# Small row blocks of the last attention layer: a second buffer for their distances, loads ahead of other steps, zeros written once, values copied a unit later

## The chip, the cores and the metric

The kernel runs on one core of one Trainium2 chip. The metric is the device time of one execution in microseconds (us), taken as the median of several runs. Beside it there is one execution recorded by the hardware profiler; durations, waits and line numbers below come from it.

## The reference, cut to what matters

The network has four layers, each of the form x = x + s * silu(g), with s from a sequence mixer and g from a feed-forward part, both fed with the layer norm of x. The kernel treats 4 sequences of 1024 tokens with 128 features. Only the last layer's code is changed (and where constants are kept), so this is the part to see:

```python
xn = _layernorm(x)
# attention, 16 heads of 8, b sequences of n tokens
qx, kx, vx = split_head(xn @ Wq.T), split_head(xn @ Wk.T), split_head(xn @ Wv.T)
ns = jnp.arange(n) + (MAXLEN - n)                    # MAXLEN = 256
ex = rel_embed[ns].reshape(n, NH, HD).transpose(1, 0, 2)
srel = srel_skew(jnp.einsum('bhnd,hmd->bhnm', qx, ex))
qk = (jnp.einsum('bhnd,bhmd->bhnm', qx, kx) + srel) * inv_dim
atten = jax.nn.softmax(qk - 1e9 * jnp.triu(jnp.ones((n, n)), 1), axis=-1)
s = jnp.einsum('bhnm,bhmd->bhnd', atten, vx).transpose(0, 2, 1, 3).reshape(b, n, d) @ Wp.T + bp
# feed-forward, 384 hidden, weights dequantised by 1/127
g = _silu((silu(xn @ wg.T) * (xn @ wu.T)) @ wd.T)
x = x + s * g
```

srel_skew shifts row n of its argument so that the entry for query n and key m depends on the embedding of their distance n - m. The position embedding has only 256 rows, so that only a band of distances needs a product of its own; the rest has one row in common.

## The kernel before, in words

The first three layers fill the span up to about 2160 us and are touched only where their constants come from. The last layer (`layer3`) runs from there to the end.

Its work is cut into units. A unit is one of 4 sequences, one group of 4 heads (i, of 4 groups) and one block of 128 query rows (t, of 8). The blocks of a group run in the order `ORDER3`, so big blocks (t over 3, with 640 to 1024 keys) and small ones (128 to 512 keys) take turns; there are 128 units, 8 to a head group. A unit's keys are cut into column tiles of 512: two for a big unit, one for a small one.

For a unit the stages are these:

- `relative3`: TensorE multiplies q with the embedding (L1914), ScalarE copies the result r out of PSUM (L1916), SyncE's queue stores it in DRAM as "flat" (L1919, L1920). This is done in parts, one part per unit, seven units ahead (`part(n + 7)`).
- `shear3`: SyncE's queue loads "flat" back with a slanted access pattern (L1935 or L1937, and L1941 for t of 3 and more), so that each row lies at its distances. GpSimd then fills what lies outside with affine selects (L1945), 1 to 3 per unit. The result is the tile "rel", with 4 heads by up to 5 blocks of 128. It is called by `ahead(n + 3)`, three units ahead. Big units take "rel" from a pool of two buffers (`p2`), small ones from a pool of one (`p1`).
- `scores3`: TensorE multiplies q and k into the score tile in PSUM (L1978), of which there is one. VectorE adds rel, scales and takes the row minimum, head by head (L1986 for columns without rel, L1993 with). ScalarE takes the exponential and the row sums (L2000).
- `transpose`: VectorE turns the weights (L1737) into "wT".
- `weigh3`: TensorE multiplies them with the values "vb" (L2014). At a group's end `finish3` scales by the row sums, and at a sequence's end `end3` projects, updates x and stores the output.

The main loop at the end of `layer3` writes the order out by hand: for each column tile the products of a later tile, pending transposes, one step of weighing, the compare of this tile; at a unit's last tile the steps listed after `continue`. Among these, `next(beside, None)` takes one step of what runs beside the attention: the gated feed-forward of the same sequence (`ffn3`: gate and up products L1861, silu L1865, copy of up L1866, their product h on GpSimd L1867, down-projection L1871, g L1872), in head group i = 1, or the beginning of the next sequence (`begin3`: layer norm, projection to q, k, v and their stores), from the fourth unit of i = 2 on. `ahead(n + 3)` comes last.

`project3` loads q and k of the next head group, into tiles of a pool of two, after a memset of q's zero column on GpSimd (L1881). `values3` loads the values as "vr" and copies them into the block-diagonal "vb" on GpSimd (L1899, four copies); `vb` is one tile, so the copies wait until the old group's last weighing has read it. Each engine carries out its instructions in the order in which they are issued, and SyncE's queue does so with DMA issues: one that waits holds back those behind it.

The constants come as one array, one transfer, in a tile kept for the whole kernel.

Of the kernel before, what the change touches and what calls it, by code (L numbers as in the profile page):

```python
# [10 lines left out]
F32 = mybir.dt.float32  # L11
# [8 lines left out]
P = 128  # L20
NB = 4
T = 1024
# [7 lines left out]
def _constants():  # L30
    i = np.arange(P)
    row, col = i[:, None], i[None, :]
    parts = []
# [4 lines left out]

    parts.append(("ident", np.eye(P)))
    parts.append(("tri", row <= col))  # L40
# [5 lines left out]

    parts.append(("sel3", (row // 32 == col // 8 % 4) & (row // 8 % 4 == col // 32)))
    parts.append(("of_a", (row // 8 % 4) == np.arange(4)[None, :]))
    parts.append(("of_t", (row % 8) == np.arange(8)[None, :]))
# [14 lines left out]
    pick = np.zeros((P, 8, P))  # L64
# [3 lines left out]
    at, where = 0, {}  # L68
# [6 lines left out]
CONST, CONST_AT = _constants()  # L75
# [12 lines left out]
def drain(gen):  # L88
    for _ in gen:
        pass  # L90


class Kit:


    def __init__(self, tc, const, const_sb):
        self.tc, self.nc = tc, tc.nc
        self.const_sb = const_sb
        self.n_copy = 0
        self.ident = self.c("ident")  # L100
        self.ident16 = const.tile([P, P], BF16, tag="ident16", name="ident16")
        self.nc.vector.tensor_copy(self.ident16, self.ident)
        self.pick = const.tile([24, 8, P], BF16, tag="pick", name="pick")

    def c(self, name):
        at, n = CONST_AT[name]
        return self.const_sb[:, at : at + n]
# [1564 lines left out]
def layer3(k, W, x3, out, eps5, ps):  # L1672
# [11 lines left out]
    nc, tc = k.nc, k.tc  # L1684
    with ExitStack() as st:
# [16 lines left out]
        def ahead(n):  # L1702
            if n < len(units):
                t = units[n][2]
                rels[n] = shear3(k, p2 if t > 3 else p1, flats[n // 8, t // 2], t)
# [5 lines left out]
        batch[0] = {}  # L1711
# [9 lines left out]
        weights, transposes, weighs, out_of = {}, [], [], {}  # L1721
# [19 lines left out]
        def weigh(n):  # L1741
            nonlocal values
            b, i, t = units[n]
            at, pair = n // 8, t // 2
            if n % 8 == 2:
                out_of[at] = ps.tile([P, 8, 32], F32, tag="o", name="po")
            o = out_of[at]
            yield from weigh3(k, weights.pop((at, pair)), vb, o, pair)
            if n % 8 == 7:
                drain(values)  # L1750
                if i == 0:
                    batch[b]["on"] = p1.tile([P, 4, 256], F32, tag="on", name="on")
                finish3(k, p1, ps, o, group[at]["sums"], batch[b]["on"][:, i, :])
                if i == 3:
                    end3(k, W, temp, ps, x3, b, batch[b], out[b])
            yield
# [12 lines left out]
        for x, (n, first) in enumerate(tiles + [(len(units), 0)] * 4):  # L1769
# [16 lines left out]
            if pos == 3 and i == 2 and b + 1 < NB:  # L1786
                batch[b + 1] = {}
                beside = begin3(k, W, p1, p2, temp, ps, dram, x3, b + 1, eps5, batch[b + 1])
# [6 lines left out]
            if pos == 6 and at + 1 < 4 * NB:  # L1795
                values = values3(k, p1, batch[(at + 1) // 4], vb, (at + 1) % 4)
                next(values)
            next(beside, None)
            ahead(n + 3)
# [76 lines left out]
def project3(k, p2, seq, i, group):  # L1876

    nc = k.nc
    q = p2.tile([P, 1 + T], F32, tag="q", name="q")
    kk = p2.tile([P, T], F32, tag="k", name="k")  # L1880
    nc.gpsimd.memset(q[:, 0:1], 0.0)  # L1881
# [192 lines left out]
def tile_kernel(ctx: ExitStack, tc: tile.TileContext, I, out):  # L2074

    nc = tc.nc
    const = ctx.enter_context(tc.tile_pool(name="const", bufs=1))
    n_const = CONST_AT["pick"][0]
    const_sb = const.tile([P, n_const], F32, tag="const_sb", name="const_sb")
    nc.sync.dma_start(out=const_sb, in_=I["const"][:, 0:n_const])  # L2080
    k = Kit(tc, const, const_sb)
# [4 lines left out]
    whole = ExitStack()  # L2086
    xp = whole.enter_context(tc.tile_pool(name="x", bufs=1, side="right"))
# [57 lines left out]
```

## Time and profile before

| what | value |
|---|---|
| median of 3 runs | 3271.13 us (3264.41 to 3277.84) |
| the profiled execution | 3261.59 us, its span 3259.9 us |
| mean granted TensorE clock | 0.734 of full speed |
| PE busy, whole span | 2317.2 us (71%) |
| VectorE busy, whole span | 2307.1 us (71%) |
| ScalarE busy, whole span | 1487.5 us (46%) |
| GpSimd busy, whole span | 1174.5 us (36%) |
| selects L1945 | 288 of 637 ns |
| memset L1881 | 16 of 99 ns |
| copies of values L1899 | 64 of 1033 ns |

A line of the timeline gives the start in us from the span's start, the duration of the group of instructions, the engine and line, the operation, what it writes and reads, the shape and the count; in brackets stands how long the engine had been idle and what ended that. "SPq" is SyncE's queue, where the duration is that of issuing a transfer. A line of the waits gives who waited for whom, the total in us, how often, and the longest. "issue" is idle time for which the trace shows no cause.

### The profile page before, as it was taken

To read this page: it belongs to the slowest core of one execution; us is meant where nothing else is said; L and a number is where in the kernel's file an instruction comes from. 1 tells how busy PE (TensorE), PEld (TensorE's weight loads), DVE (VectorE), ACT (ScalarE), POOL (GpSimd) and SP (SyncE) were. 2 spreads that over 40 slices of the span, in tenths; PEclk is the share of its full clock that TensorE was granted. 3 is DMA by queue.
4 is the path that set the end of the run, shared out by engine and by line. 5 is a ranking of instruction groups with operands and counts; after the bars stand their busy time and mean duration, and the time that the engine had idled before them with its cause. 6 is when DMAs were issued, how large, how long until landed. Compare 5 with 4: busy or idle time off the path is not lost. (4 is left out here: it accounts for less than half of the span.)

```text
span 3259.9 us, 50636 instructions
## 1 busy us (share of the span) xinstructions
PE 2317.2 (71%) x18321; PEld 1327.2 (41%) x18321; DVE 2307.1 (71%) x5534; ACT 1487.5 (46%) x3248; POOL 1174.5 (36%) x1104
## 2 busy tenths in 40 slices
PE   5787777677776777965533772557888888888885
PEld 2555555222322323651101222344545555555553
DVE  5555545878878886657868878437678778777786
ACT  4555453433333334344322561125665665755663
POOL 3344334144444444224577222332322322323322
PEclk9888888678788888985555666566766766756676
DMA  3000000100000000320433444347677677766772
GB/s 89 3 1 1 1 1 1 35 0 0 0 0 1 0 0 33 105 84 0 111 95 105 109 108 99 110 119 209 187 213 207 181 209 217 202 195 193 200 231 71
DMA packets 396446, 303.46 MB, mean 93 GB/s; under 512 B 96272, under 2 KB 380812, under 8 KB 390564
## 3 DMA queue, kind: packets, MB, share of 16 engines
q1 hardware_dynamic: 395044, 296.03, 32.2%
q10 hardware_dynamic: 1152, 4.19, 0.4%
q8 instruction: 144, 2.36, 0.3%
q14 instruction: 106, 0.87, 0.1%
HBM read 160.63 MB, written 138.94 MB: 92 GB/s over the span
## 5 line engine op out<-in xcount | busy, mean ns | idle before, releaser
L2000 ACT ACTIVATE neg<-neg,low 128x640 f32<-128x640 f32 (+7 forms) x512 | 390.0, 763 | 153.9 <-DVE low L1993 153.8
L1945 POOL TENSOR_SCALAR_AFFINE_SELECT rel<-rel 128x512 f32<-128x512 f32 x288 | 179.9, 637 | 565.6 <-DMA rel<-flat 357.3
L1737 DVE STREAM_TRANSPOSE wT<-neg 128x640 f32<-128x640 f32 (+7 forms) x512 | 362.0, 753 | 7.6 <-ACT neg L2000 6.9
L1978 PE MATMUL score<-k,q 8*128 8x512 f32 (+3 forms) x1536 | 295.0, 747 | 91.2 <-DVE low L1993 91.0
L1993 DVE CUSTOM_DVE_ANT_0 neg<-score,rel,low 128x128 f32<-128x128 f32 (+3 forms) x448 | 217.5, 516 | 152.5 <-PE score L1978 105.6
L1914 PE MATMUL pr<-emb,q 8*128 8x256 f32 x1024 | 245.2, 569 | 45.0 <-ACT r L1916 27.2
L2014 PEld LDWEIGHTS po<-wT,vb 128*32 128x32 f32 x10240 | 208.1, 140 | 143.3 <-issue 78.0
L2014 PE MATMUL po<-wT,vb 128*32 128x64 f32 (+1 forms) x10240 | 242.9, 259 | 31.7 <-issue 17.3
L1914 PEld LDWEIGHTS pr<-emb,q 8*128 8x128 f32 x1024 | 153.6, 269 | 124.4 <-ACT r L1916 62.9
L1916 ACT COPY r<-pr 128x512 f32<-128x512 f32 x256 | 138.4, 581 | 144.2 <-PE pr L1914 95.1
L1993 DVE CUSTOM_DVE_ANT_0 neg<-score,rel 128x512 f32<-128x512 f32 (+3 forms) x320 | 149.3, 520 | 26.7 <-issue 15.4
L1978 PEld LDWEIGHTS score<-k,q 8*128 8x128 f32 x1536 | 103.0, 249 | 153.9 <-DVE low L1993 127.8
L835 PE MATMUL pg<-xnT,w 128*128 128x512 f32 x256 | 148.4, 663 | 7.7 <-DVE h L839 4.5
L214 PE MATMUL pt<-ident,three 128*24 128x128 bf16 x64 | 9.2, 295 | 201.9 <-DVE three L211 201.9
L788 POOL TENSOR_TENSOR prod<-rest,kv 128x2048 f32<-128x2048 f32 x32 | 145.6, 4599 | 18.4 <-ACT rest L778 18.4
L837 PE MATMUL pu<-xin,w 128*128 128x512 f32 x256 | 140.5, 632 | 14.3 <-DVE h L839 7.9
L826 PE MATMUL po<-h,w 128*128 128x512 f32 x256 | 129.6, 627 | 27.1 <-DVE h L839 27.1
L838 ACT ACTIVATE h<-pg 128x512 f32<-128x512 f32 x128 | 75.9, 595 | 156.2 <-PE pg L835 152.7
L1986 DVE TENSOR_SCALAR_CACHE_REDUCE neg<-score 128x384 f32<-128x384 f32 (+2 forms) x192 | 79.7, 415 | 69.3 <-PE score L1978 69.3
L1050 PE MATMUL ph<-xin,upT 128*128 128x512 bf16 (+1 forms) x128 | 71.3, 588 | 78.5 <-DVE xin L1044 77.7
L1455 PE MATMUL read<-kt,const_sb 128*128 128x128 f32 x256 | 50.1, 366 | 94.2 <-POOL kt L1450 94.2
L431 PE MATMUL px<-hT,xbcT 128*128 128x512 f32 x256 | 115.4, 595 | 0.0
(621 smaller groups left out, 5690.5 us busy)
## 6 DMA issues: line engine op xcount, KB each, us to landing
flat<-r SPq DMA_DIRECT2D x256, 256.0 KB
rel<-flat SPq DMA_DIRECT2D x112, 512.0 KB
flat<-r SPq DMA_DIRECT2D x256, 128.0 KB
rel<-flat SPq DMA_DIRECT2D x96, 256.0 KB
kt<-kd SPq DMA_DIRECT2D x16, 512.0 KB
qt<-qd SPq DMA_DIRECT2D x16, 512.0 KB
kdc<-kdd SPq DMA_DIRECT2D x16, 512.0 KB
ktc<-ktd SPq DMA_DIRECT2D x16, 512.0 KB
```

The costliest lines, as they stand in the source:

```text
L788: nc.gpsimd.tensor_tensor(prod, attn.rearrange("p (t h g) -> p t h g", t=4, g=16)[:, t].unsqueeze(2).to_broadcast(each), kv[:, t, 1, :].re ...
L826: nc.tensor.matmul(po, W["w2"][:, e, c, :], h[:, c, :], start=(e == 0 and c == 0), stop=(e == 7 and c == 1))
L835: nc.tensor.matmul(pg, W["w1"][:, e, c * P : (c + 1) * P], xnT, start=True, stop=True)
L837: nc.tensor.matmul(pu, W["w3"][:, e, c * P : (c + 1) * P], xin, start=True, stop=True)
L1737: nc.vector.transpose(weights[at, pair][j][:, t % 2, 0 : (t + 1) * P], S[j][:, 0 : (t + 1) * P])
L1914: nc.tensor.matmul(to[:, m, :], q[at, t * P : (t + 1) * P], W["emb"][at, i, :], start=True, stop=True)
L1916: nc.scalar.copy(r[:, n], to)
L1945: nc.gpsimd.affine_select(out=rel[:, :, slot(back), :], in_=rel[:, :, slot(0), :], compare_op=op, fill=fill, base=0, pattern=[[0, 4], [-si ...
L1978: nc.tensor.matmul(sc[:, j, 0 : last - first], q[at(j), 1 + t * P : 1 + n], kk[at(j), first:last], start=True, stop=True)
L1993: nc.vector.tensor_tensor_reduce(out=neg[:, begin:last], in0=sc[:, j, begin - first : last - first], in1=rel[:, j, slot : slot + (last - b ...
L2000: nc.scalar.activation(neg[:, 0:n], neg[:, 0:n], AF.Exp, bias=here, scale=-1.0, accum_out=group["sums"][:, j, t : t + 1])
L2014: nc.tensor.matmul(o[32 * j : 32 * j + 32, 2 * pair + m.start : 2 * pair + 2, :], vb[:, kb, j].rearrange("p a d -> p (a d)"), weights[j][: ...
```

## The change

It has five parts.

- The constants are put in another order and loaded in two transfers. The first 268 columns, which the last layer needs, stay for the whole kernel (`last_sb`). The other 1080 columns lie in the pool of x, which is given back ahead of the last layer.
- Small units take "rel" from the pool of two buffers as well.
- q has two fixed tiles (`qs`); their zero column is written once, at the start of the layer.
- `ahead(n + 3)` is called before `next(beside, None)` rather than after it.
- The copies of the next group's values are no longer issued where the old group's last weighing ends, but kept in a list (`ripe`) and issued at the end of the current unit, behind `ahead` (or when the next group's weighing starts).

```diff
@@ -36,17 +36,18 @@
         a = np.asarray(a, np.float32)
         return np.ascontiguousarray(np.broadcast_to(a.reshape(1, -1), (P, a.size)))
 
+
     parts.append(("ident", np.eye(P)))
+
+    parts.append(("sel3", (row // 32 == col // 8 % 4) & (row // 8 % 4 == col // 32)))
+    parts.append(("of_a", (row // 8 % 4) == np.arange(4)[None, :]))
+    parts.append(("of_t", (row % 8) == np.arange(8)[None, :]))
     parts.append(("tri", row <= col))
     parts.append(("neg_ssd", np.where(col >= row, 0.0, -1e30)))
     parts.append(("tril", col < row))
     parts.append(("bd8", np.kron(np.eye(16), np.ones((8, 8)))))
     parts.append(("bd16", np.kron(np.eye(8), np.full((16, 16), 1.0 / 16.0))))
     parts.append(("ones", np.ones((P, P))))
-
-    parts.append(("sel3", (row // 32 == col // 8 % 4) & (row // 8 % 4 == col // 32)))
-    parts.append(("of_a", (row // 8 % 4) == np.arange(4)[None, :]))
-    parts.append(("of_t", (row % 8) == np.arange(8)[None, :]))
     parts.append(("sel16", (row // 16) == np.arange(8)[None, :]))
 
     parts.append(("rep8", np.where(row < 8, (col % 8) == row, 0.0)))
@@ -93,9 +94,9 @@
 class Kit:
 
 
-    def __init__(self, tc, const, const_sb):
+    def __init__(self, tc, const, const_sb, last_sb):
         self.tc, self.nc = tc, tc.nc
-        self.const_sb = const_sb
+        self.const_sb, self.last_sb = const_sb, last_sb
         self.n_copy = 0
         self.ident = self.c("ident")
         self.ident16 = const.tile([P, P], BF16, tag="ident16", name="ident16")
@@ -104,7 +105,8 @@
 
     def c(self, name):
         at, n = CONST_AT[name]
-        return self.const_sb[:, at : at + n]
+        n_last = CONST_AT["tri"][0]
+        return self.last_sb[:, at : at + n] if at < n_last else self.const_sb[:, at - n_last : at - n_last + n]
 
     def copy(self, out, in_):
 
@@ -1702,13 +1704,16 @@
         def ahead(n):
             if n < len(units):
                 t = units[n][2]
-                rels[n] = shear3(k, p2 if t > 3 else p1, flats[n // 8, t // 2], t)
+                rels[n] = shear3(k, p2, flats[n // 8, t // 2], t)
 
         def stream():
             for n, (b, i, t) in enumerate(units):
                 yield from scores3(k, p1, p2, ps, group[n // 8], rels.pop(n), t)
 
-        batch[0] = {}
+        qs = [p1.tile([P, 1 + T], F32, tag=f"q{n}", name="q") for n in range(2)]
+        for q in qs:
+            nc.gpsimd.memset(q[:, 0:1], 0.0)
+        batch[0] = {"qs": qs}
         drain(begin3(k, W, p1, p2, temp, ps, dram, x3, 0, eps5, batch[0]))
         group[0] = {}
         drain(project3(k, p2, batch[0], 0, group[0]))
@@ -1718,7 +1723,12 @@
         for n in range(3):
             ahead(n)
         beside, project, values = iter(()), iter(()), iter(())
-        weights, transposes, weighs, out_of = {}, [], [], {}
+        weights, transposes, weighs, out_of, ripe = {}, [], [], {}, []
+
+        def fill_values():
+
+            while ripe:
+                drain(ripe.pop())
 
         def transpose(n, heads):
 
@@ -1739,15 +1749,15 @@
                 weighs.append((big, weigh(n)))
 
         def weigh(n):
-            nonlocal values
             b, i, t = units[n]
             at, pair = n // 8, t // 2
             if n % 8 == 2:
+                fill_values()
                 out_of[at] = ps.tile([P, 8, 32], F32, tag="o", name="po")
             o = out_of[at]
             yield from weigh3(k, weights.pop((at, pair)), vb, o, pair)
             if n % 8 == 7:
-                drain(values)
+                ripe.append(values)
                 if i == 0:
                     batch[b]["on"] = p1.tile([P, 4, 256], F32, tag="on", name="on")
                 finish3(k, p1, ps, o, group[at]["sums"], batch[b]["on"][:, i, :])
@@ -1784,7 +1794,7 @@
             if pos == 0 and i == 1:
                 beside = ffn3(k, W, p1, temp, ps, batch[b])
             if pos == 3 and i == 2 and b + 1 < NB:
-                batch[b + 1] = {}
+                batch[b + 1] = {"qs": qs}
                 beside = begin3(k, W, p1, p2, temp, ps, dram, x3, b + 1, eps5, batch[b + 1])
             if pos == 0:
 
@@ -1795,8 +1805,9 @@
             if pos == 6 and at + 1 < 4 * NB:
                 values = values3(k, p1, batch[(at + 1) // 4], vb, (at + 1) % 4)
                 next(values)
+            ahead(n + 3)
+            fill_values()
             next(beside, None)
-            ahead(n + 3)
         while weighs:
             step()
 
@@ -1876,9 +1887,8 @@
 def project3(k, p2, seq, i, group):
 
     nc = k.nc
-    q = p2.tile([P, 1 + T], F32, tag="q", name="q")
+    q = seq["qs"][i % 2]
     kk = p2.tile([P, T], F32, tag="k", name="k")
-    nc.gpsimd.memset(q[:, 0:1], 0.0)
     group.update({"q": q, "k": kk, "sums": p2.tile([P, 4, NT], F32, tag="sums", name="sums")})
     for n, dst in ((0, q[:, 1:]), (1, kk)):
         for j in range(4):
@@ -2075,16 +2085,18 @@
 
     nc = tc.nc
     const = ctx.enter_context(tc.tile_pool(name="const", bufs=1))
-    n_const = CONST_AT["pick"][0]
-    const_sb = const.tile([P, n_const], F32, tag="const_sb", name="const_sb")
-    nc.sync.dma_start(out=const_sb, in_=I["const"][:, 0:n_const])
-    k = Kit(tc, const, const_sb)
+    whole = ExitStack()
+    xp = whole.enter_context(tc.tile_pool(name="x", bufs=1, side="right"))
+    n_last, n_const = CONST_AT["tri"][0], CONST_AT["pick"][0]
+    last_sb = const.tile([P, n_last], F32, tag="last_sb", name="last_sb")
+    nc.sync.dma_start(out=last_sb, in_=I["const"][:, 0:n_last])
+    const_sb = xp.tile([P, n_const - n_last], F32, tag="const_sb", name="const_sb")
+    nc.sync.dma_start(out=const_sb, in_=I["const"][:, n_last:n_const])
+    k = Kit(tc, xp, const_sb, last_sb)
     eps5 = const.tile([P, 1], F32, tag="eps5", name="eps5")
     nc.vector.memset(eps5, 1e-5)
     store = ctx.enter_context(tc.tile_pool(name="x3", bufs=1, space=DRAM))
     x3 = store.tile([P, NB * NT, D], F32, tag="x3", name="x3")
-    whole = ExitStack()
-    xp = whole.enter_context(tc.tile_pool(name="x", bufs=1, side="right"))
     x_all = xp.tile([P, NB * NT, D], F32, tag="x_all", name="x_all")
 
     right = ExitStack()
```

## The prediction

> **What bounds the kernel now.** First the totals of the fourth layer's stretch (busy time of PE, weight load, VectorE, ScalarE, GpSimd, then granted clock, DMA share, GB/s):
>
> ```profile
> 2200.00:3260.00 1060.00, 875.55 (x13307) 549.51 (x13305) 809.56 (x2556) 628.43 (x1478) 295.66 (x418) 0.68 0.67 193
> ```
>
> No engine is full: PE is busy 83%, VectorE 76%, GpSimd 28%. So the waits of the same stretch come next (engine and its instruction, what it waited for: us, times, longest):
>
> ```profile
> SPq L1935 <- DVE low L1993: 226.9, 81, 11.0
> SPq L1937 <- DVE low L1993: 31.8, 12, 4.9
> ...
> POOL rel L1945 <- DMA rel<-flat: 357.3, 73, 15.5
> ...
> DVE neg L1993 <- PE score L1978: 111.3, 59, 9.7
> PE score L1978 <- DVE low L1993: 91.0, 85, 10.6
> ...
> POOL q L1881 <- PE score L1978: 49.4, 10, 7.8
> POOL h L1867 <- ACT up L1866: 46.9, 26, 8.1
> ...
> DVE neg L1993 <- issue: 42.5, 18, 6.8
> ...
> PE pr L1914 <- ACT r L1916: 27.0, 27, 3.9
> ...
> DVE neg L1993 <- POOL rel L1945: 13.9, 1, 13.9
> ```
>
> Read them by who needs whom. PE's scores and VectorE's compare wait for each other (111.3 and 91.0 us: one PSUM buffer), and that loop sets the pace. SP's load of distances waits 258.7 us for a compare to free its buffer, and GpSimd's select waits 357.3 us for loads, but the compare waited for a select once: 13.9 us, in the first unit of the layer, which this change does not reach. GpSimd idles because its next work isn't there; the path does not go through it.
>
> **Is the select ever late?** I set each select's end against the start of the compare that reads it, unit by unit. After the first unit the slack is never below 2.4 us; the median is 8.2 for small units (t up to 3), 16.7 for big ones. The closest, unit 37:
>
> ```profile
> 2503.97 0.46 SPq L1935 DMA_DIRECT2D rel<-flat  x1
> 2508.56 1.34 POOL L1945 TENSOR_SCALAR_AFFINE_SELECT rel<-rel 128x512 f32<-128x512 f32 x2 [13.49 <-DMA rel<-flat]
> 2512.34 0.56 DVE L1993 CUSTOM_DVE_ANT_0 neg<-score,rel 128x384 f32<-128x384 f32 x1 [2.15 <-issue]
> ```
>
> Load issued at 2503.97, both selects done at 2509.90, compare at 2512.34: slack 2.44 us. The last line's 2.15 us have no cause in the trace, and not the select.
>
> **The change part by part.**
>
> *Second buffer for small units.* Before, the load for unit n+3 waited until unit n+1 had been compared; now it needs n-1's end and never stands. Small units' part of the 258.7 us is some 121 us of SP. Gain on the path: 0, since the selects it makes earlier were 2.4 us early at worst. If that cover were gone, a late select would cost its lateness one to one. Behind these waits on SP stand the stores of r (L1919, L1920). They leave earlier, and ScalarE's copy of r (L1916), whose buffer they free, waited for them 3.3 us in all: I credit 0, with 3 as the other end. At "Best Practices" in the Trainium skill's page Trainium Kernel Development and Optimization stands: double-buffer, so that transfers overlap compute. It would credit this edit with up to the 121 us. The row speaks otherwise: three loads are in flight already and the compare waited for none after the first. By the rule 3271 - 121 = 3150; by the row 3271. I take the row.
>
> *Memsets.* 16 of 0.099 us become 2. GpSimd stood 49.4 us at this memset (for the old scores to be done with q), but behind it stood only selects with slack and the products h, which wait for ScalarE (46.9 us). Gain 0 (bound 2).
>
> *Copies of values a unit later.* Four of 1.03 us per group move from the group's end behind the selects that `ahead` issues. Nobody waited for them: they ended about 4.3 us after the old group's last product, and the new group's first product came at least 6.3 us later. A unit lasts about 8 us (64.5 us for a group of 8), so part of the slack of the tightest groups (3 and 7) is eaten. But the wait they had at GpSimd (76.3 us for PE's products) is gone too. Cost 0, at most 4 x 1.03 in two groups, 8.
>
> *Loads and selects ahead of the other steps.* The steps are the gated FFN (four per batch, in its second head group) and the next batch's beginning. Counts do not change: 208 load issues, 288 selects. On SP the small loads (0.4 to 0.5 us, two for t = 3) now precede a step's x and qk transfers, which have most of a group to spare. On GpSimd the products h now stand behind selects. The FFN's first step, before (issue lines and start, duration, engine):
>
> ```profile
> 2532.91 0.51 SPq L1935 DMA_DIRECT2D rel<-flat  x1
> ...
> 2535.65 0.94 ACT L1866 COPY up<-pgu 128x256 f32<-128x256 f32 x3
> ...
> 2536.12 2.10 POOL L1867 TENSOR_TENSOR h<-h,up 128x256 f32<-128x256 f32 x3 [2.19 <-ACT up L1866]
> ...
> 2538.16 1.94 POOL L1945 TENSOR_SCALAR_AFFINE_SELECT rel<-rel 128x512 f32<-128x512 f32 x3
> 2538.27 1.16 PE L1871 MATMUL po<-downT,h 128*128 128x128 f32 x8 [0.20 <-POOL h L1867]
> 2540.57 0.50 PE L1978 MATMUL score<-k,q 8*128 8x128 f32 x8
> ```
>
> After, the built order is h, two selects, h, one select, h, so the third h comes 3 x 0.64 = 1.9 us later, less some 0.6, because ScalarE's order becomes h, up, h, up and the first product starts sooner. PE's last down-projection follows about 1.3 us later, and so do the scores at 2540.57 queued behind it, for which the next compare waits. The FFN's second step is bound by PE and ScalarE and takes back a part: +0.8 us net per batch, in three batches, +2.4 (0 to 2.5 each, 0 to 7.5). That needs unit 42's load to be in by then: issued at 2532.91 before, earlier after, with some 3 us to land, it is in before the first up. Steps two and three find selects whose loads came long ago. At step four the three products stand behind unit 47's select; its load follows stores of r that are out well before the up copies at 2574, 4 us of room: 0.
>
> *Batch 0.* The units after its second group's start see another order on PE: the next scores stand ahead of the FFN's products rather than behind, which removes a VectorE gap of 4.6 us at unit 12 and gives most of it back at the next tile: -2.7 (-5 to 0).
>
> *Start of the next batch.* In the third group, VectorE's transposes now stand ahead of the layer norm's statistics:
>
> ```profile
> 2631.34 0.74 DVE L1737 STREAM_TRANSPOSE wT<-neg 128x256 f32<-128x256 f32 x2
> 2631.41 5.44 PE L2014 MATMUL po<-wT,vb 128*32 128x64 f32 x201 [0.54 <-DVE ln_mv L137]
> ...
> 2639.30 0.48 DVE L1993 CUSTOM_DVE_ANT_0 neg<-score,rel,low 128x256 f32<-128x256 f32 x1 [2.46 <-PE score L1978]
> ```
>
> PE's stream of weighted sums starts earlier by the 0.26 + 0.17 + 0.26 + 0.17 us of statistics and what goes with them, about 0.9, and the scores behind it as well, for which VectorE stood 2.46 us: -0.9 in each of three batches, -2.7 (-3 to 0). Behind the statistics waits the normalising of x, which has until the next batch.
>
> *Constants in two transfers.* One more issue of 0.4 us on SP ahead of all other loads: +0.4 (0 to 1).
>
> Sum: 2.4 - 2.7 - 2.7 + 0.4 = -2.6 us. The profiled execution took 3261.59 us (span 3259.9, 1.7 around it), so about 3259. The runs' median, 3271.13, lies 9.5 above it, so I forecast 3271.1 - 2.6 = 3268.5, stated as 3268.
>
> **Rivals.**
>
> *Faster: SP's blocked queue is a hidden brake.* For it: 258.7 us of waits in the one queue that also carries the stores, and two rows whose cause may be late loads or stores: compares of small units that waited for nothing visible (15.1 of the 42.5 us "issue") and PE's projections waiting for ScalarE's r (27.0). Against: selects with 2.4 us of slack, and 3.3 us of r waiting for stores. All of it recovered would be 42 us, 3229; half of it, 3250, is this rival's time.
>
> *Slower: a product h stuck behind a select whose load has not landed.* GpSimd is in order, so the down-projection waits, and PE's scores behind it, and the compare. It decides where the load lands after ScalarE's up copies: later than 2535.9 for unit 42, later than 2574.5 for unit 47. Then a step loses what the four stores ahead (4 x 0.5), the landing (3.0) and two selects (1.3) leave: some 6 us, once per batch, 24: 3295. Against it: on the old timeline the loads are 2 to 4 us ahead, and the freed SP queue should widen that.
>
> *The loads do not move.* SP is in order, and its stores wait 146.7 us for ScalarE's r; the loads may sit behind these instead. The edits then do nothing: 3271.
>
> **How the numbers follow.** Forecast 0.57, loads that do not move 0.13, faster 0.14, slower 0.16. A measurement of this kernel tells 0.5% (16 us) from no change; the first two cases lie inside: faster 0.14, same 0.70, slower 0.16. The range runs from the faster rival's 3250 to just under the slower one's, 3293, leaving out half of each; the forecast's own range, with the ends of the sums (-13 to +17, most unlikely together), is 3258 to 3280.
>
> **What would show it.** Right: SP's waits at L1935 and L1937 for the compare fall by about half; the memset's 49.4 us vanish; small units' selects end a unit's length (8 us or so) earlier before their compare; PE's and VectorE's waits for each other stay within a few us of 111 and 91; groups with FFN steps change by 1 or 2 us. Wrong: L1871 waiting for h far above its 16 + 2.4 us (the slower rival), or VectorE's idle time in the layer down by tens of us (the faster one).

## The result: 0.43% slower

The changed kernel takes 3277.07 us (median of 20 runs, 3265.78 to 3285.65), the kernel before 3260.82 us in the same series (median of 20, 3252.27 to 3278.53). The ratio is 1.0043, with a 95% interval of 1.0029 to 1.0057: some 14 us slower (the two medians themselves lie 16.3 us apart). The profiled execution took 3272.36 us, its span 3270.2 us, 10.3 more than before.

TensorE does no more work than before. The totals of the changed kernel's last layer, in the columns of the first line of the prediction:

```profile
2200.00:3270.00 1070.00, 874.22 (x13311) 548.27 (x13308) 809.25 (x2556) 630.39 (x1480) 294.98 (x404) 0.69 0.70 192
```

It is busy 874.2 us (875.6 before) and idle 195.8 us (184.5 before), so what was added is idle time.

The waits of the changed kernel in the last layer, which starts at the same place and ends some 10 us later (line numbers are shifted by 10: L1945 is the load of distances, L2003 the compare, L1988 the scores, L2024 the weighed sums, L1878 the products h). First SyncE's queue, then the engines:

```profile
SPq L1945 <- DVE low L2003: 172.9, 54, 11.2
```

```profile
POOL rel L1955 <- DMA rel<-flat: 394.8, 70, 15.3
DVE neg L2003 <- issue: 129.1, 57, 8.8
...
PE score L1988 <- DVE low L2003: 92.9, 78, 11.7
...
PEld po L2024 <- issue: 90.6, 105, 3.4
...
POOL h L1878 <- ACT up L1877: 33.7, 21, 8.6
DVE neg L2003 <- POOL rel L1955: 31.3, 6, 15.4
PE pr L1924 <- ACT r L1926: 27.0, 25, 4.0
...
PE po L2024 <- issue: 24.4, 18, 3.3
...
DVE neg L2003 <- PE score L1988: 10.2, 11, 2.2
```

What was meant to happen did: SyncE's wait for the compare fell from 258.7 to 172.9 us, the memset's wait is gone, and small units' selects end 18.7 us (median) ahead of their compare rather than 8.2, after the first unit never less than 7.9. None of that shortened the time. The row of compares that waited for a select (31.3 us) is no late select beyond its longest wait, 15.4 us in the first unit of the layer: before each of the other five compares the scores had ended only 0.16 to 0.18 us earlier, so they had waited for the scores. Two rows moved that the reading of the profile before had passed over.

First, the compare's wait changed its name. Before, it was 111.3 us for TensorE's scores and 42.5 without a cause; now it is 10.2 and 129.1, and the 15.9 us of those five compares belong to it too. The sum is nearly the same (153.8 and 155.2), so this looks like bookkeeping. The compare's own view says what it is. Of the kernel before:

```profile
L1993 DVEq EVENT_SEMAPHORE  x198: 21/21/7165, 2194.8 to 3232.7; - x198
```

and of the kernel after (instruction of VectorE's sequencer, count, duration ns min/median/max):

```profile
L2003 DVEq EVENT_SEMAPHORE  x237: 21/330/9328, 2195.9 to 3242.0; - x119
```

These are waits put into instructions of their own, since a compare in the built program carries one wait at most. Before, most of them are over at once (median 21 ns): where a compare waits long for the scores, it mostly does so itself. After, they last (median 330 ns): the wait for the scores has moved into them, and the compare carries its wait for GpSimd. That costs time. From the end of the last score product to the start of a compare that had waited for it over 0.5 us, the median is 69 ns before (75 cases) and 165 ns after (74 cases).

Second, TensorE stands longer where the trace gives no cause, between two weighed sums. That row was "PE po L2014 <- issue: 17.3, 19, 1.9" before; it is 24.4 us, with single gaps up to 3.3. The largest gap, in unit 52 (timeline of the kernel after):

```profile
2637.78 1.33 PE L2024 MATMUL po<-wT,vb 128*32 128x64 f32 x79
2642.40 0.32 PE L2024 MATMUL po<-wT,vb 128*32 128x64 f32 x9 [3.29 <-issue]
2642.65 0.71 PE L1988 MATMUL score<-k,q 8*128 8x256 f32 x8
2643.29 1.58 PE L2024 MATMUL po<-wT,vb 128*32 128x32 f32 x102
2643.54 0.48 DVE L2003 CUSTOM_DVE_ANT_0 neg<-score,rel,low 128x256 f32<-128x256 f32 x1 [2.23 <-PE score L1988]
```

and the transfers from 2636 to 2643 us (busy tenths and GB/s in 40 slices of 0.175 us, then packets by queue):

```profile
DMA  9225788999999999999999999611001100000000
GB/s 47 18 105 176 146 246 211 339 404 392 383 357 345 360 336 325 278 228 301 195 154 115 124 143 116 54 12 18 7 10 10 10 12 1 0 0 0 0 0 0
...
q8 instruction: 1, 0.02, 1.4%
```

Queue 8 brings TensorE's instructions: over the whole kernel it moves 144 packets of 16 KB (2.36 MB), 64 bytes for each of TensorE's some 36,900 instructions. In this window it brings one, from 2639.18 to 2640.80, as the burst of loads ends; TensorE runs dry at 2639.1 and goes on at 2642.4, when the transfers have been quiet for over a microsecond. All gaps of this kind over 0.6 us in the last layer (17 in the kernel after) end 1.2 to 1.7 us after such a packet. Counted in TensorE's instructions they lie a multiple of 256 apart, within one, and 256 instructions of 64 bytes are a packet of 16 KB.

### The profile page after: what moved, and what is told of

It is laid out like the page before. It is cut to its first block, busy times and chain, and to the rows that moved or that the text cites. A ratio compares the mean times of both kernels' runs of the same rounds, so it can differ in the third digit from the quotient of the medians.

```text
span 3270.2 us, 50707 instructions
## 1 busy us (share of the span) xinstructions
PE 2314.5 (71%) x18319; PEld 1325.2 (41%) x18321; DVE 2308.7 (71%) x5534; ACT 1487.9 (45%) x3248; POOL 1175.1 (36%) x1090
## 3 DMA queue, kind: packets, MB, share of 16 engines
q8 instruction: 144, 2.36, 0.3%
## 5 line engine op out<-in xcount | busy, mean ns | idle before, releaser
L1747 DVE STREAM_TRANSPOSE wT<-neg 128x640 f32<-128x640 f32 (+7 forms) x512 | 361.0, 753 | 13.4 <-ACT neg L2010 7.5
L1988 PE MATMUL score<-k,q 8*128 8x512 f32 (+3 forms) x1536 | 291.9, 746 | 93.5 <-DVE low L2003 92.9
L2003 DVE CUSTOM_DVE_ANT_0 neg<-score,rel,low 128x128 f32<-128x128 f32 (+3 forms) x448 | 218.0, 517 | 164.0 <-issue 118.3
L2024 PE MATMUL po<-wT,vb 128*32 128x64 f32 (+1 forms) x10240 | 239.8, 257 | 38.7 <-issue 24.4
L2024 PEld LDWEIGHTS po<-wT,vb 128*32 128x32 f32 x10240 | 205.7, 139 | 150.4 <-issue 90.6
L2003 DVE CUSTOM_DVE_ANT_0 neg<-score,rel 128x512 f32<-128x512 f32 (+3 forms) x320 | 149.3, 521 | 22.8 <-issue 10.9
L1988 PEld LDWEIGHTS score<-k,q 8*128 8x128 f32 x1536 | 101.5, 250 | 154.3 <-DVE low L2003 126.5
L1457 PE MATMUL read<-kt,last_sb 128*128 128x128 f32 x256 | 49.3, 362 | 94.3 <-POOL kt L1452 94.3
```

What stands on the lines that cost most here:

```text
L1747: nc.vector.transpose(weights[at, pair][j][:, t % 2, 0 : (t + 1) * P], S[j][:, 0 : (t + 1) * P])
L1988: nc.tensor.matmul(sc[:, j, 0 : last - first], q[at(j), 1 + t * P : 1 + n], kk[at(j), first:last], start=True, stop=True)
L2003: nc.vector.tensor_tensor_reduce(out=neg[:, begin:last], in0=sc[:, j, begin - first : last - first], in1=rel[:, j, slot : slot + (last - b ...
L2024: nc.tensor.matmul(o[32 * j : 32 * j + 32, 2 * pair + m.start : 2 * pair + 2, :], vb[:, kb, j].rearrange("p a d -> p (a d)"), weights[j][: ...
```

## The experiments

Times are ratios to the kernel before on the same chip in the same series, with 95% intervals. "Standing" is TensorE's row for weighed sums without a cause (17.3 us before, 24.4 after), "step" the median from scores to waiting compare. Both come from one profile each. The single execution that a profile shows lies anywhere in the spread of its runs (some 20 us), so the ratio decides and the rows only name the place. The granted clock does not tell the kernels apart: averaged over its runs it is 0.735 for the kernel before and the one after, 0.736 for a_buffer and 0.734 for a_order.

| kernel | small buffers | ratio | standing us | step ns |
|---|---|---|---|---|
| b_const | 1 | 0.9996 (0.9982 to 1.0011) | 18.6 | 70 |
| a_buffer | 1 | 1.0004 (0.9990 to 1.0017) | 16.9 | 69 |
| b_small_late | 1 | 1.0014 (1.0004 to 1.0024) | 16.1 | 69 |
| before_touch2 | 1 | 1.0002 (0.9987 to 1.0018) | 17.8 | 68 |
| after | 2 | 1.0043 (1.0029 to 1.0057) | 24.4 | 165 |
| a_order | 2 | 1.0036 (1.0025 to 1.0047) | 28.6 | 165 |
| a_fix | 2 | 1.0035 (1.0022 to 1.0047) | 22.3 | 164 |
| b_const_buffer | 2 | 1.0053 (1.0038 to 1.0068) | 28.4 | 165 |
| a_small_late | 2 | 1.0029 (1.0018 to 1.0041) | 20.9 | 165 |
| a_small_early | 2 | 1.0062 (1.0042 to 1.0081) | 17.0 | 165 |
| a_hold | 2 | 1.0077 (1.0050 to 1.0104) | 23.3 | 164 |
| a_touch2 | 2 | 1.0036 (1.0023 to 1.0049) | 22.9 | 68 |
| a_fix_touch2 | 2 | 1.0027 (1.0013 to 1.0041) | 21.9 | 68 |
| a_no_small | 2, hardly used | 1.0000 (0.9985 to 1.0015) | 10.3 | 164 |
| b_dummy | 1 | 1.0151 (1.0124 to 1.0178) | 34.9 | 163 |
| a_touch | 2 | 1.0139 (1.0113 to 1.0166) | 19.5 | 68 |
| before_touch | 1 | 1.0129 (1.0105 to 1.0153) | 15.0 | 68 |

### Which part of the change: four single edits

*a_buffer*: the kernel after with one buffer for small units.

```diff
-                rels[n] = shear3(k, p2, flats[n // 8, t // 2], t)
+                rels[n] = shear3(k, p2 if t > 3 else p1, flats[n // 8, t // 2], t)
```

> The kernel after, but small units take their distances from the pool of one buffer again; everything else of the change stays. Theory 1 (the second buffer makes the selects of the big unit 42, 74, 106 ready so early that they are built in between the three products h of the first feed-forward step, which delays the down-projection and the scores behind it): most of the loss goes, ratio to before 1.0000 to 1.0015. Theory 2 (the order of loads and steps does it, as the prediction had it): the loss stays, 1.0035 to 1.0050. Theory 3 (neither: shifted phases of the TensorE clock and the start of the layer): anything, but the products h uninterrupted.

Measured 1.0004: the loss is gone. The constants, the order of the calls, the fixed q tiles and the later copies of values are all still in, so together they cost nothing that can be measured.

*a_order*: the kernel after with the steps called ahead of the loads again.

```diff
-            ahead(n + 3)
-            fill_values()
             next(beside, None)
+            ahead(n + 3)
+            fill_values()
```

> The kernel after, with the step beside (feed-forward, next batch's beginning) called ahead of the loads again, as before the change. Theory 1 (second buffer): the products h stay interrupted by selects and the loss stays, ratio to before 1.0035 to 1.0050. Theory 2 (order): the loss goes, 1.0000 to 1.0015.

Measured 1.0036: the loss stays. In the built program GpSimd's and ScalarE's order are the same as after, the products h still interrupted by selects; with one buffer (a_buffer) they are not interrupted, though the calls stand as after. So this interruption, which the prediction put down to the order of the calls, is the second buffer's doing; presumably, unit 42's load no longer stands behind unit 41's, its selects are ready sooner, and they are built in ahead of h.

*a_fix*: the kernel after, with h uninterrupted.

```diff
+            if i == 0 and pos == 7:
+                fill_values()
+            elif i == 1 and pos == 0:
+                next(beside, None)
+                ahead(n + 2)
+                ahead(n + 3)
+                fill_values()
+            else:
                 ahead(n + 3)
                 fill_values()
                 next(beside, None)
```

> The kernel after with one thing more: at the start of the second head group, where the first feed-forward step stands, the load and the selects of the unit two ahead are issued behind that step and not one unit earlier, so that GpSimd multiplies h three times without a select in between. Second buffer, order, memsets and copies of values stay. Theory 1: most of the loss goes, some 10 us of 14, ratio to before 1.0000 to 1.0015. Theory 2 or 3: the loss stays, 1.0035 to 1.0050.

Measured 1.0035. TensorE's wait for h (its matmul row) went from 5.5 to 3.8 us, so the edit did its work, and the loss stayed. Theory 1, that the interrupted products are most of it, is wrong.

*b_const*: the kernel before with the constants as after (the change's part of the constants alone).

> The kernel before with the new order of the constants and the two transfers alone; everything else as before. All theories: only the later start, +0.8 us at the end of the third layer in the profile, ratio 1.0000 to 1.0008. If the place of the constants or of the layer's tiles in memory matters: 1.002 or more.

Measured 0.9996: nothing, as expected.

### The second buffer alone, and the moment of its loads

*b_const_buffer*: b_const and the first line of a_buffer's diff the other way round.

> The kernel before with the constants in two transfers (without which the memory does not suffice) and the second buffer for small units; order of the calls, memsets and copies of values as before the change. Theory 4 (the second buffer alone: small loads leave earlier, and their traffic makes TensorE's instruction fetches, 16 KB each, come late in the streams of weighed sums): ratio to before 1.0025 to 1.0045, TensorE's gaps of over 0.9 us without a cause in the trace between two weighed sums 18 to 26 us together, against 10 to 13 with one buffer. Rival (it needs buffer and changed order together): 0.9990 to 1.0010.

Measured 1.0053: the second buffer alone is enough. TensorE's gaps over 0.9 us between weighed sums are 27.0 us together, 13.2 in b_const.

*a_small_late* and *a_small_early*: the kernel after, with the small unit's load moved.

```diff
-            ahead(n + 3)
+            for m in (n + 2, n + 3):       # a_small_early: (n + 4, n + 3)
+                if m < len(units) and (units[m][2] > 3) == (m == n + 3):
+                    ahead(m)
             fill_values()
```

> The kernel after, with two buffers, but the load of a small unit is issued a unit later, at the end of the small unit before it rather than of the big one: about when one buffer let it go before, yet without SyncE's queue standing. Theory 4a (the moment of the small loads counts): the loss goes, 0.9990 to 1.0015, gaps without a cause 10 to 14 us. Theory 4b (that the queue no longer stands, so stores and big loads leave sooner): the loss stays, 1.0025 to 1.0045, gaps 18 or more.

> The kernel after, with the load of a small unit issued at the end of a small unit, like in the run with later loads, but two units earlier still (four units ahead, into the buffer just read). If the place within the cycle of a big and a small unit counts (4a): the loss goes, 0.9990 to 1.0015. If every load that leaves earlier than in the kernel before costs, or SyncE's queue going ahead (4b): 1.0025 or more.

Measured 1.0029 and 1.0062: the loss stays. But the edits hardly moved the loads, since the order in the program is not the order of the calls. A small unit's load was issued 13.4 us (median) ahead of its first compare before and 26.5 after; in a_small_late it is 24.6, in a_small_early 28.2. So 4a, that the moment of the loads counts, is neither shown nor refuted. The gaps over 0.9 us were 15.5 and 12.0 us; the second is as low as with one buffer although that kernel is among the slowest, but its profiled execution (span 3263.7) is far below its own median of 3286.04, so its rows say little.

*b_small_late*: one buffer, load moved as in a_small_late. It was meant to keep SyncE's queue from standing.

> The kernel before with the constants in two transfers and one buffer, but the load of a small unit issued at the end of the small unit before it, when the buffer is free or nearly so: SyncE's queue hardly stands for it. Theory 4b (what costs is that the queue goes ahead): the loss appears without any second buffer, ratio to before 1.0025 to 1.0055, TensorE's gaps without a cause between weighed sums 15 us or more. Theory 5 (the second buffer itself, by where tiles lie or how they are waited for): 0.9985 to 1.0010.

*a_hold*: the kernel after, with SyncE's queue made to stand.

```diff
+            if n + 3 < len(units) and units[n + 3][2] < 4:
+                hold = dram.tile([1, 1], F32, tag="hold", name="hold")
+                nc.sync.dma_start(out=hold, in_=group[(n + 1) // 8]["low", units[n + 1][2]][3][0:1, 1:2])
             ahead(n + 3)
```

> The kernel after, two buffers, with one transfer of 4 bytes ahead of each small load: it reads the last compare's minimum of the small unit before, so SyncE's queue stands until that compare, as it did with one buffer. Theory 4b: the loss goes, 0.9990 to 1.0015, gaps without a cause 10 to 14 us, SyncE's waits for the compare back to some 240 us. Theory 5: the loss stays, 1.0030 to 1.0055.

Measured 1.0014 and 1.0077. b_small_late did not do what was meant: its queue still waited 253.0 us for compares (258.7 before), and its small loads left 13.6 us ahead of the compare, as before. Its 4.6 us have another likely source: three compares (units 37, 69 and 101) started 0.03 us after their select ended and 1.0 to 2.0 us after their scores, 4.1 us in all. In a_hold the queue stood 259.6 us, as long as before, and the loss did not go but grew. That speaks against theory 4b, that the queue going ahead is what costs. It is no clean refutation: the small loads still left 22.7 us ahead of the compare, and the edit adds transfers, for which 59 compares wait in the built program.

### More and less traffic

*b_dummy*: b_const, with a load that nobody reads.

```diff
+    if 0 < t < 4:
+        more = pool.tile([P, 4, 2, P], F32, tag="more", name="more")
+        nc.sync.dma_start(out=more.rearrange("p n s c -> p n (s c)"), in_=shear(256))
```

> The kernel before with the constants in two transfers, one buffer, and for small units of t = 1 to 3 the 512 KB load issued a second time into a tile that nobody reads (48 loads, 24.6 MB more). If traffic holds up the instruction fetches: gaps without a cause up by 5 us or more over the 13 of the kernel with the constants alone, and time up by 5 to 25 us, ratio 1.0015 to 1.0075, without any select coming late. If the loads are only waited for by selects and these have slack: 0.9990 to 1.0010.

Measured 1.0151, 50 us, twice the upper end of what was expected. The gaps over 0.9 us rose to 31.7 us (by 18.5). The kernel isn't clean, though: its compares have the longer step (163 ns) as well, and some start within 0.25 us of the end of a select. It shows the direction, not the size. Its rows of the waits in the last layer (those of the run with less traffic follow below):

```profile
PEld po L2019 <- issue: 95.0, 108, 3.4
...
PE po L2019 <- issue: 34.9, 21, 3.3
```

*a_no_small*: the kernel after without the small units' transfers. It leaves out the loads and selects of small units from the second head group on.

```diff
-                rels[n] = shear3(k, p2, flats[n // 8, t // 2], t)
+                if t > 3 or n < 8:
+                    rels[n] = shear3(k, p2, flats[n // 8, t // 2], t)
+                    if n == 7:
+                        fixed.append(rels[n])
+                else:
+                    rels[n] = fixed[0]
```

> The kernel after, but small units of all head groups except the first leave out their loads and selects and use the distances of one earlier small unit (60 loads, some 26 MB, and 105 selects less; the small blocks' scores are then not the reference's). The compares of the big units' second tiles still wait for the scores by way of a wait instruction (165 ns), so only traffic, fetches and the select queue change. Theory of fetches: TensorE's standing without a cause falls from 28 us to below 20 and the ratio to before to 0.9960 to 1.0010. Theory of the step alone: the loss stays, 1.0030 to 1.0050.

```profile
PEld po L2029 <- issue: 72.8, 95, 1.9
...
PE po L2029 <- issue: 10.3, 13, 1.7
```

Measured 1.0000 (within 5 us): the 14 us are gone, with the step still at 164 ns. It took out 75 loads, 31.5 MB and 90 selects, not the 60, 26 and 105 that were expected. TensorE's waits without a cause, over all its matrix products, fell from 26.4 to 10.8 us (18.2 in the kernel before). The edit also leaves h uninterrupted and makes 60 compares of small units wait for the scores themselves, so the 14 us are not the price of the transfers alone. The tiles lie at the same addresses as in the kernel after, so their place in memory is not what costs. The kernel before is as fast while it has all these transfers and 7 us more of such waits; the one thing known that it has in exchange is the shorter step.

### The step from scores to compare

Why does one more buffer give the compares another wait? With one buffer a small unit's selects come behind those of the next big unit, which is compared later. The small unit's compare has then waited for GpSimd far enough, and the big unit's second tile needs no wait for GpSimd of its own: in the built program 59 compares wait for the scores themselves. With two buffers the selects come in the order of the units, the first compare of each of the 192 column tiles carries a wait for GpSimd, and none waits for the scores itself.

*a_touch*, *before_touch*: a copy ahead of each unit's compares, in the kernel after and before.

```diff
+        if first == 0:
+            seen = p2.tile([P, 1], F32, tag="seen", name="seen")
+            nc.vector.tensor_copy(seen, rel[:, 0, min(t, 4), 0:1])
```

> The kernel after, with one VectorE copy of a single column per unit ahead of its compares, which reads the last part of the distances that the selects write. It waits for GpSimd there, so the compares behind it need no wait for GpSimd of their own and wait for TensorE's scores themselves (140 of them in the built program, none in the kernel after, 59 before). Theory 6 (with the second buffer a small unit's selects are built ahead of the next big unit's, so every compare needs a wait for GpSimd as well, and its wait for the scores is put into a separate wait instruction, from whose end the compare starts 165 ns after the scores rather than 69): the step from the scores' end to the waiting compare is back to some 70 ns, and the ratio to before falls to 0.9985 to 1.0015. Rival (only fetches and traffic count): step of 70 ns, but ratio 1.0025 to 1.0045.

> The kernel before with the same copy of a single column per unit. Theory 6: 59 compares that wait for the scores themselves become 140; those added are mostly small units, which seldom wait for the scores: ratio 0.9970 to 1.0000. If the 128 copies cost more than they save: 1.0000 to 1.0030.

Measured 1.0139 and 1.0129. The step is 68 ns, but the copies, which depend on nothing but the select, were built far ahead of their place, and VectorE stands there (view of the copy's line in a_touch):

```profile
L1994 DVE COPY seen<-rel x128: 94/146/156, 2209.4 to 3257.0; 128x1 f32<-128x1 f32 x128
...
  POOL rel L1955: 88.2, 45
```

That is 88.2 us of new standing, so the experiment failed. With the copy in both, the kernels with one and with two buffers are 0.10% apart, their intervals wider than that; it settles nothing.

*a_touch2*: tied to its place, between the tiles of a big unit; *before_touch2* is the same in the kernel before.

```diff
+            if j == 3 and last < n:
+                seen = p2.tile([P, 1], F32, tag="seen", name="seen")
+                nc.vector.tensor_tensor(seen, rel[:, 0, min(t, 4), 0:1], here, ALU.add)
```

> The kernel after, with one small VectorE addition per big unit between its two column tiles: it reads the last part of the distances and the minimum just found, so it can't be built earlier, and waits for GpSimd there. The second tile's compare then waits for TensorE's scores itself (64 in the built program, none in the kernel after). Theory 6: the step from the scores' end to the waiting compare falls from 165 to 70 ns, some 74 times, 7 us; with PE's products starting that much sooner 7 to 12 us in all: ratio to before 1.0000 to 1.0025. Rival (fetches and traffic alone): 1.0035 to 1.0055.

> The kernel before with the same 64 small additions between the two tiles of a big unit. There most second tiles wait for the scores themselves already (59 of the compares, 70 with the additions), so it shows what the additions cost by themselves: ratio 0.9990 to 1.0010 if they lie in VectorE's idle time; 1.0015 to 1.0035 if they are on the path, and then the run after with them has gained more than it shows.

*a_fix_touch2*: this and a_fix.

> The same small addition, and with it the products h of the first feed-forward step built without selects in between (load and selects of the unit two ahead issued behind that step). Theory 6 with the prediction's term for that step (TensorE's standing for h 3.4 us more than with one buffer): 0.9990 to 1.0015.

Measured 1.0036, 1.0002 and 1.0027. The step is 68 ns again, yet only 0.07% is regained, within the intervals; with h uninterrupted too, 0.16%, short of what was expected. The step's 96 ns times 74 waiting compares, 7.1 us, is what it could have given; the runs show 2 us and can't tell that from none or from the whole. The test is not clean either: the additions show no cost in the ratio of before_touch2, but TensorE's wait for the compare rose with them, from 91.0 to 101.6 us there and from 92.9 to 107.8 in a_touch2. Some 9 us of the loss are left in a_fix_touch2, where TensorE's standing is still 21.9 us.

### What is settled and what is open

Settled: the second buffer for small units makes the loss, alone and whole (a_buffer, b_const_buffer). It isn't a late select: in the kernel after, no select ends less than 5.0 us ahead of its compare after the first unit.

Measured beside it: a step 96 ns longer in all kernels with two buffers but the two that were given additions; more standing of TensorE between weighed sums in 8 of 9 (20.9 to 28.6 us against 16.1 to 18.6; the exception is a_small_early); and a wait for h of 3.8 to 8.3 us against 2.4 to 4.8. From 2200 us to its end the layer took 14.0 us longer, on average, in the seven profiles with two buffers and no addition than in the four with one (before, b_const, a_buffer, b_small_late). In TensorE's rows of the waits this is 6.3 us more standing between weighed sums, 5.2 more waiting for the compare and 2.4 for h; 2.2 is more busy time, and the other rows lose 2.1. That says where TensorE stood, not what each would give back if it were taken away.

Leaving out the small units' loads and selects gives back all of it. Open is how the 14 us divide by cause, why TensorE's packets come later with two buffers, and whether the earlier moment of the small loads is the reason: no run had two buffers and the loads at the old moment. None of these kernels is measurably faster than the kernel before.

## Why the prediction was wrong

The number, 3268, lies between the two medians of the series, 3260.82 and 3277.07; its sign was wrong. Against the 3271.13 of three runs shown, the forecast was 2.6 us faster; the kernel before is really at 3261, so 10 us of the distance to the measured time were compensated by chance.

- **Slack of the selects, and 0 for the second buffer's gain: right.** The waits of SyncE fell by a third (86 us; the forecast said half, 121), the selects of small units have 10 us more slack, and no time was gained by it. The page Trainium Kernel Development and Optimization in the Trainium skill, whose "Best Practices" would have double-buffered, is not borne out here: the loads were overlapped already.
- **The second buffer's "Gain on the path: 0" was the step that failed.** That no gain came was right, but the term was put at nothing in both directions, and the runs showed a cost in its place: 14 us in the whole change, 17 alone (b_const_buffer, 1.0053). The buffer was costed by what it removes (a wait in a queue) and never by what it adds: another order of selects on GpSimd, which puts a wait between the scores and the compares (69 to 165 ns) and interrupts the products h, and loads that leave 13 us earlier, with TensorE standing 7 us longer for its instructions. How the cost divides among these is open. The order could be read from the built program. TensorE's standing could be seen in the profile before as "PE po <- issue", 17.3 us, and was not asked about.
- **The first feed-forward step: size about right, cause wrong.** +2.4 us (0 to 7.5) was forecast. TensorE's matmuls stood 5.5 us for h in the profile after against 2.4; unit 41 took 1.6 us more in the profile of after. But a_order shows that it comes with the buffer, not with the order of the calls.
- **Batch 0 and the next batch's beginning, -2.7 each: not shown.** Group 1 took 67.7 us rather than 73.0, but in b_const, which has the old order, it took 67.0. Unit 52 with the one behind it took 0.2 us less, unit 84 with its follower 1.4 less; a_buffer and b_const are as fast as before, so no sum of gains shows in the runs.
- **Constants, +0.4: right**, +0.8 us at the end of the third layer in the profile, nothing in b_const's time.
- **Memsets and values, 0: right**, by a_buffer, which contains both and is at 1.0004.
- **The slower rival** had the right side and the wrong mechanism and size: it wanted 24 us from products h behind late loads, and TensorE's matmuls waited 5.5 us for h in all. "Loads that do not move" is refuted by the slack.
- **What would show it** named TensorE's and VectorE's waits for each other, to stay within a few us. They stayed in sum: TensorE's 92.9 us, VectorE's 155.2 once its rows are put together. The signal was the change of name from "PE score" to "issue" that no point of the list looked for.

## What to carry to other kernels

A further buffer also changes the order in which a planner places instructions and the waits they carry, so cost it by the built program's order and waits, not only by the wait that it takes away. A late wait that sat in an instruction of its own started the next one 96 ns later here; what that is worth in time these runs do not show. An experiment that moves a call has to be read in its own trace first: four of the edits above moved the small loads by 4 us or less, where the second buffer had moved them by 13. And idle time of TensorE without a cause in the middle of a stream of small matrix products, at even distances in instructions, was here a packet of instructions that came late.

## What the runs showed of the hardware that was not expected

TensorE ran dry of instructions between 16 KB packets, for 0.6 to 3.8 us at a time; from a packet's end to its next product it took 1.2 to 1.7 us. The later packets can be seen in all traces. From the start of the instruction that stands 60 ahead of a packet's first one to the start of that packet's transfer, the median in the last layer is 2.6 to 2.8 us in the five kernels with one buffer (before and the table's first four), 2.9 to 3.4 in the nine with two, 2.2 in a_no_small and 4.0 in b_dummy. That data transfers hold the packets up is what these last two suggest; within one trace the link is weak (a rank correlation of 0.25 to 0.39, in eight kernels, with the busy share of the DMA engines 1 to 3 us after that point).

An instruction of VectorE with two operands in SBUF was held by one of GpSimd (a_touch2; the addition takes 160 ns in the median):

```profile
2489.70 2.34 POOL L230 TENSOR_TENSOR x<-x,s 128x1024 f32<-128x1024 f32 x1
...
2489.84 2.22 DVE L2011 TENSOR_TENSOR seen<-rel,low 128x1 f32<-128x1 f32 x1
2491.98 0.60 DVE L2003 CUSTOM_DVE_ANT_0 neg<-score,rel,low 128x384 f32<-128x384 f32 x1
```

The single-column addition lasts 2.22 us (so in 3 of 64) and ends with GpSimd's update of x. The Trainium skill, page SBUF — State Buffer, section "SBUF: two separate sides", says that such a pair shares a port which the first to come holds for its whole instruction; this trace agrees. The compares, with one operand in PSUM, ran beside selects at their usual length (128x256 in the kernel before: 482 ns beside a select, 480 without).

The granted clock of TensorE changes between 1.0 and 0.5 in the last layer of both traces, and each stretch lasts a multiple of 3.4 us. Unit 72 took 12.4 us in the profile before and 16.2 after, 3.8 of the 10.3 us between the two spans: before, TensorE was at full clock from its start on; after, at half clock for its first 8 us. In a_order, as slow as the kernel after, it took 12.6 us. Such differences of single places between two profiles need not be the change's, and a comparison of places needs several profiles of each kind.
